# The tightest width table of the AUGRU: one line or two

## The chip, the cores and the metric

The kernel runs on one core of one Trainium2 chip. The metric is the device time of one execution in microseconds (us), the median of several runs. The kernel before takes 2072.88 us (three runs, 2072.65 to 2073.33). One execution was also recorded by the hardware profiler; its span, from the first to the last instruction, is 2067.4 us.

## What is computed

The reference scores 1024 users, each with a history of up to 100 items of 128 numbers. A GRU runs over all 100 steps of every history, an attention over the GRU's states gives one weight per user and step, and a second recurrence, the AUGRU, runs over the GRU's states with these weights. A small network makes one score of the AUGRU's state at the last real step of the user. Cut to the part that matters here:

```python
def augru_step(h, inp):
    x_t, a_t = inp
    ti = jnp.concatenate([h, x_t], axis=-1)
    r = jax.nn.sigmoid(ti @ aug_Wr.T + aug_br)
    u = jax.nn.sigmoid(ti @ aug_Wu.T + aug_bu)
    h_hat = jnp.tanh(jnp.concatenate([h * r, x_t], axis=-1) @ aug_Wh.T + aug_bh)
    u = a_t[:, None] * u
    h_new = (1.0 - u) * h + u * h_hat
    return (h_new, h_new)
...
idx = (sequential_length - 1).astype(jnp.int32)[:, None, None]
attention_feature = jnp.take_along_axis(aug_out, idx, axis=1)[:, 0, :]
```

Only the state at step `sequential_length - 1` is read. A user whose history has 40 items needs no AUGRU step after the fortieth. The lengths are drawn evenly from 1 to 100, so the number of users still alive falls by about 10 per step.

## The kernel before, in words

All data are f32, and the 128 features lie on the partitions. The users are two halves of 512 columns. The kernel has two phases.

The first phase (`gru_phase`, the first 1450 us) does the GRU, the attention and the sums over the history, step by step for both halves. Between its steps a generator, `load_later`, does small preparations one piece at a time. One of them ranks the users by length. The AUGRU then takes users in order of falling length, dealt alternately to the two halves, so that the living users are always the first columns of both halves.

The second phase (`augru_phase`, from about 1450 us to the end) is the AUGRU. Its loop runs over t from 1 to 99 and over the two halves i. Each turn (`half_step`) works on the first `widths[t]` columns of its half. Per turn TensorE does six matmuls of that width: three that open the gates of a turn to come with the GRU states (L1044) and three that close gates with the state or the reset state (L1048). ScalarE does three activations (L1056, L1068, L1069), VectorE five elementwise operations (L1072, L1074, L1076, L1082, L1085) and one transpose of the keys for t+2 in blocks of 32 columns (L1034). Steps 0 to 7 get their keys through TensorE transposes instead (L1030). The order of all instructions is written out by hand.

The keys of later steps come by indirect DMA from GpSimd (`load_rows`, L164). Eight steps are fetched at a time, in blocks of 32 columns, as many as cover the width at the first of the eight steps. Each fetch is preceded by a one-column copy (L163) that waits for a result of the loop and so paces the fetches. `spread` deals the fetches of the next eight steps over the turns before them. As groups of 64 columns die, `predict(g)` does the last network for them; its pieces run between the turns.

The widths are constants of the program. They come from a straight line that lies above the number of living users:

```python
EIGHTH, FALL, LEAST = 8, 41, 96
SPARE = (10, 40)
ROOM = [[EIGHTH * (HB + n) - FALL * t for t in range(T)] for n in SPARE]
ALIVE = [[min(HB, 2 * -(-r // (2 * EIGHTH))) for r in room] for room in ROOM] + [[HB] * T]
WIDTHS = [[max(LEAST, n) for n in alive] for alive in ALIVE]
```

A line is kept in eighths of a column: it starts `n` columns above 512 and falls 41/8 columns a step. The width is the line's value rounded up to an even number, at most 512 and at least 96. There are three tables: room for 10 more columns per half, room for 40, and full width. The program holds the whole AUGRU three times, once per table. `load_later` counts the living users of every step with eight small matmuls (L311), compares the counts with both lines, which GpSimd wrote with two iota instructions (L274), and stores a number, `over`. After the first phase the kernel loads it and branches (L1246 on) to the tightest table whose line lies nowhere below the count.

Of the kernel before, what the change touches and what calls it, by code (L numbers as in the profile page):

```python
# [9 lines left out]
F32 = mybir.dt.float32  # L10
BF16 = mybir.dt.bfloat16
I32 = mybir.dt.int32
# [9 lines left out]
T = 100  # L22
HB = 512
NH = B // HB
# [35 lines left out]
GATHER = 70  # L60


EIGHTH, FALL, LEAST = 8, 41, 96
SPARE = (10, 40)
ROOM = [[EIGHTH * (HB + n) - FALL * t for t in range(T)] for n in SPARE]
ALIVE = [[min(HB, 2 * -(-r // (2 * EIGHTH))) for r in room] for room in ROOM] + [[HB] * T]
WIDTHS = [[max(LEAST, n) for n in alive] for alive in ALIVE]

# [6 lines left out]
def kernel(ctx: ExitStack, tc: tile.TileContext, a: dict, out: bass.AP):  # L75
# [26 lines left out]
    nc = tc.nc  # L102
# [9 lines left out]
    over_d = dram.tile([1, 1], I32, name="over_d")  # L112
# [63 lines left out]
    def gru_phase(pools):  # L176
# [10 lines left out]
        pre = pools.enter_context(tc.tile_pool(name="pre", bufs=1))  # L187
# [52 lines left out]
        def load_later():  # L240
# [28 lines left out]
            ids = pre.tile([P, NG, 2], I32, name="ids")  # L269
            nc.gpsimd.iota(ids[:, :, 0], pattern=[[P, NG]], base=0, channel_multiplier=1)  # L270
            rooms = []
            for n in SPARE:
                rooms.append(pre.tile([1, T], I32, name=f"room_i{n}"))
                nc.gpsimd.iota(  # L274
                    rooms[-1],
                    pattern=[[-NH * FALL, T]],
                    base=NH * EIGHTH * (HB + n),
                    channel_multiplier=0,
                )
            yield  # L280
            length = pre.tile([P, NG], F32, name="length")
            nc.scalar.copy(length, len_i)
# [2 lines left out]
            own = pre.tile([P, NG], F32, name="own")  # L285
            nc.scalar.copy(own, ids[:, :, 0])
            room = []
            for n, room_i in zip(SPARE, rooms):
                room.append(pre.tile([1, T], F32, name=f"room{n}"))
                nc.scalar.copy(room[-1], room_i)  # L290
            yield

# [17 lines left out]
            for g in range(NG):  # L310
                nc.tensor.matmul(  # L311
                    count, lhsT=ones, rhs=alive[:, g, :], start=g == 0, stop=g == NG - 1
                )
            over = pre.tile([1, len(SPARE)], F32, name="over")
            for j in range(len(SPARE)):
                nc.vector.scalar_tensor_tensor(
                    out=room[j],
                    in0=count,
                    scalar=float(EIGHTH),
                    in1=room[j],  # L320
                    op0=ALU.mult,
                    op1=ALU.is_gt,
                )
                nc.vector.tensor_reduce(over[:, j : j + 1], room[j], AX.X, ALU.max)
# [12 lines left out]
                pattern=[[1, B]],  # L337
                base=0,
                channel_multiplier=0,
# [300 lines left out]
        def blocked(t):  # L640
            return t.rearrange("p (k r) -> p k r", r=R)
# [156 lines left out]
        def nothing():  # L798
            pass

        rest = load_later()
        early = [load_rows(0, i, HB, mid) for i in range(NH)]
        more_early = [load_rows(1, i, HB, kx) for i in range(NH)]

        late, again, early_from = 6, 24, 84
        for s in range(T):
            last = s == T - 1
            n, due = divmod(s - again, 4)
            n, i = divmod(n, NH)
# [85 lines left out]
        n = ENDS[-3] - ENDS[-4] + 1  # L895
# [33 lines left out]
        for half in reversed(halves):  # L929
            t = blocked(s_bs[NH * (soft["j"] % 2) + half.i])  # L930
# [311 lines left out]
        with ExitStack() as pools, tc.manual_schedule():  # L1242
            augru_phase(pools, WIDTHS[n], ALIVE[n])

    over = nc.values_load(over_d, min_val=0, max_val=len(SPARE))
    with tc.If(over < 1) as fits:  # L1246
        augru(0)
    with fits.Else():
# [70 lines left out]
```

## Time and profile before

| what | value |
|---|---|
| median time | 2072.88 us |
| profiled span | 2067.4 us |
| TensorE (PE) busy | 2029.8 us, 98% |
| VectorE (DVE) busy | 1755.2 us, 85% |
| GpSimd (POOL) busy | 1304.8 us, 63% |
| ScalarE (ACT) busy | 831.5 us, 40% |
| DMA | 99 GB/s on average |
| mean granted TensorE clock | 0.996 |
| first turn of the AUGRU loop starts | 1466.92 us |
| last turn of the AUGRU loop (t=99, second half) starts | 2054.11 us |

Busy time is the time in which an engine had at least one instruction in work. The ends of matmuls are modelled and neighbours overlap, so the busy share of PE does not say how near PE is to its limit; the distance between the starts of matmuls does. PEld is TensorE's loading of weights, which runs beside the matmuls. Each f32 matmul appears in the trace as two records, each with its own weight load. In the group lists, "+47 forms" means that other shapes are averaged in.

### The profile page before, as it was taken

The numbers are of one execution on the slowest core, as the hardware profiler recorded it, in microseconds if no ns is written. First come the engines' busy times: TensorE is split into PE (matmuls) and PEld (weight loads), VectorE is DVE, ScalarE is ACT, GpSimd is POOL, SyncE is SP. The second block draws the span as 40 slices with busy tenths as digits, with TensorE's granted clock in tenths as the row PEclk, the third lists the DMA queues.
The fourth block names the chain that finished last, engine by engine and source line by source line (L and its number), as shares of the span: only waits on it lengthen the run. The fifth ranks groups of instructions, "written<-read, shape, count | busy, mean of one in ns | idle before, by whom it ended". The sixth has DMA issues, their size and how long they took to land. (4 is left out here: it accounts for less than half of the span.)

```text
span 2067.4 us, 26811 instructions
## 1 busy us (share of the span) xinstructions
PE 2029.8 (98%) x8320; PEld 978.9 (47%) x8320; DVE 1755.2 (85%) x3050; ACT 831.5 (40%) x1516; POOL 1304.8 (63%) x1306
## 2 busy tenths in 40 slices
PE   8999999999999999999999999997899999999997
PEld 3343333333333333333333333333444556679997
DVE  6888999998989898988889899999467777888886
ACT  3334343333434343334334343343344444445554
POOL 0234939669796959595987767998545434444332
PEclk9999999999999999999999999999999999999999
DMA  4543333323334333333432332333434333333332
GB/s 119 116 93 94 98 103 97 102 80 88 110 111 101 112 114 113 105 111 102 122 97 77 95 104 88 103 104 104 113 103 110 98 91 98 94 97 102 88 75 36
DMA packets 254324, 205.09 MB, mean 99 GB/s; under 512 B 75814, under 2 KB 216842, under 8 KB 254170
## 3 DMA queue, kind: packets, MB, share of 16 engines
q1 hardware_dynamic: 240266, 170.64, 29.6%
q0 software_dynamic: 12320, 32.44, 5.7%
q8 instruction: 68, 1.11, 0.2%
q14 instruction: 86, 0.70, 0.1%
q10 hardware_dynamic: 1584, 0.20, 0.1%
HBM read 147.16 MB, written 54.40 MB: 97 GB/s over the span
## 5 line engine op out<-in xcount | busy, mean ns | idle before, releaser
L495 PE MATMUL ps<-x,wih 128*128 128x512 f32 x1200 | 592.1, 603 | 4.0 <-DMA x<-in_hist_x 4.0
L495 PE MATMUL ps<-hn,whh 128*128 128x512 f32 x1188 | 574.4, 592 | 0.0
L495 PEld LDWEIGHTS ps<-x,wih 128*128 128x128 f32 x1200 | 220.7, 190 | 327.1 <-issue 251.4
L495 PEld LDWEIGHTS ps<-hn,whh 128*128 128x128 f32 x1188 | 225.7, 190 | 284.1 <-issue 276.0
L481 POOL TENSOR_TENSOR xm<-x,m 128x512 f32<-128x512 f32 x200 | 247.1, 1236 | 136.3 <-DMA m<-mask_d 136.0
L526 ACT ACTIVATE ps<-ps,bih 128x512 f32<-128x512 f32 x200 | 132.4, 662 | 488.7 <-DVE ps L525 488.7
L507 ACT ACTIVATE r<-ps,brz 128x512 f32<-128x512 f32 x200 | 137.4, 687 | 371.1 <-PE ps L495 370.2
L482 POOL TENSOR_TENSOR hist<-hist,xm 128x512 f32<-128x512 f32 x200 | 266.6, 1333 | 15.7
L594 POOL TENSOR_TENSOR pooled<-pooled,kw 128x512 f32<-128x512 f32 x191 | 254.3, 1332 | 15.0
L593 POOL TENSOR_TENSOR kw<-kt,e 128x512 f32<-128x512 f32 x191 | 219.1, 1147 | 64.7 <-DVE e L766 64.6
L164 POOL DMA_INDIRECT rows<-keys_d,idx_k x208 | 202.0, 971 | 82.2 <-POOL rows L163 52.7
L570 DVE TENSOR_TENSOR kq<-hn,item 128x512 f32<-128x512 f32 x200 | 228.5, 1182 | 0.0
L657 PE MATMUL pm<-hn,wk 128*32 128x512 f32 x1200 | 211.9, 596 | 3.7 <-ACT q L238 2.2
L657 PE MATMUL pm<-kq,wkq 128*32 128x512 f32 x1200 | 209.5, 592 | 0.0
L1056 ACT ACTIVATE c<-ph,bh 128x96 f32<-128x96 f32 (+42 forms) x198 | 96.7, 489 | 257.1 <-PE ph L1048 227.4
L657 PE MATMUL pm<-mv,w 128*32 128x512 f32 (+1 forms) x808 | 196.3, 598 | 1.4 <-DVE e L747 1.4
L163 POOL COPY rows<-rest 128x1 f32<-128x1 f32 x208 | 39.1, 188 | 210.1 <-DVE rest L1085 205.0
L691 DVE TENSOR_TENSOR f<-pm,q 128x512 f32<-128x512 f32 x200 | 128.4, 683 | 50.5 <-PE pm L657 50.4
L1072 DVE TENSOR_TENSOR pu<-pu,c 128x96 f32<-128x96 f32 (+42 forms) x197 | 88.8, 451 | 92.9 <-ACT c L1056 80.3
L530 DVE TENSOR_TENSOR d<-hn,ps 128x512 f32<-128x512 f32 x198 | 136.1, 687 | 34.9 <-ACT ps L526 32.5
L525 DVE TENSOR_TENSOR ps<-ps,u 128x512 f32<-128x512 f32 x200 | 140.0, 700 | 21.6 <-PE ps L495 0.5
L531 DVE TENSOR_TENSOR d<-ps,d 128x512 f32<-128x512 f32 x200 | 138.3, 691 | 23.5 <-ACT ps L527 6.5
(180 smaller groups left out, 3024.5 us busy)
## 6 DMA issues: line engine op xcount, KB each, us to landing
x<-in_hist_x SPq DMA_DIRECT2D x212, 256.0 KB
keys_d<-kt SPq DMA_DIRECT2D x46, 1024.0 KB
m<-mask_d SPq DMA_DIRECT2D x200, 128.0 KB
keys_d<-kt SPq DMA_DIRECT2D x64, 64.0 KB
rows<-keys_d,idx_k POOLq DMA_INDIRECT x208
s_b<-mv SPq DMA_DIRECT2D x200, 8.0 KB
mask_i<-in_mask SPq DMA_DIRECT2D x8, 200.0 KB
at<-att_d SPq DMA_DIRECT2D x32, 48.0 KB
```

The lines of the kernel that those rows point to most:

```text
L164: nc.gpsimd.indirect_dma_start(out=r[:, k, :], out_offset=None, in_=keys_d[q], in_offset=bass.IndirectOffsetOnAxis(ap=idx_k[:, k, i : i + ...
L481: nc.gpsimd.tensor_mul(d, x, m)
L482: nc.gpsimd.tensor_add(acc, acc, d)
L495: nc.tensor.matmul(p, lhsT=w[:, g, :], rhs=v, start=(j == 0), stop=(j == len(parts) - 1),)
L507: nc.scalar.activation(r, pr, AF.Sigmoid, bias=brz[:, 0:1])
L525: nc.vector.tensor_add(pi, pi, u)
L530: nc.vector.tensor_sub(d, h, pi)
L531: nc.vector.tensor_mul(d, pz, d)
L570: nc.vector.tensor_mul(kq, h, item[:, self.cols])
L593: eng.tensor_mul(d, k, w)
L594: eng.tensor_add(acc, acc, d)
L657: nc.tensor.matmul(p[i][s, :], lhsT=w[:, s], rhs=v, start=start, stop=stop)
```

## The change

The tightest table is made of two lines instead of one. From step 0 the first line starts only 2 columns above 512 and falls 38/8 columns a step. From step 16 on a second line takes over, the old one moved down from 10 to 8 columns of room. The second table (40 columns) and the third stay. The purpose is to spend fewer columns on users that have ended. The lines are written by GpSimd as before, now with one iota per piece. Two columns of room for both halves together are what is left at the tightest place: at step 56, 464 of the given users are alive and the two halves have 466 columns of line.

```diff
-EIGHTH, FALL, LEAST = 8, 41, 96
-SPARE = (10, 40)
-ROOM = [[EIGHTH * (HB + n) - FALL * t for t in range(T)] for n in SPARE]
+EIGHTH, LEAST = 8, 96
+
+LINES = (((0, 2, 38), (16, 8, 41)), ((0, 40, 41),))
+ROOM = [
+    [max((t0, EIGHTH * (HB + n) - fall * t) for t0, n, fall in lines if t0 <= t)[1] for t in range(T)]
+    for lines in LINES
+]
 ALIVE = [[min(HB, 2 * -(-r // (2 * EIGHTH))) for r in room] for room in ROOM] + [[HB] * T]
...
             rooms = []
-            for n in SPARE:
-                rooms.append(pre.tile([1, T], I32, name=f"room_i{n}"))
-                nc.gpsimd.iota(
-                    rooms[-1],
-                    pattern=[[-NH * FALL, T]],
-                    base=NH * EIGHTH * (HB + n),
-                    channel_multiplier=0,
-                )
+            for j, lines in enumerate(LINES):
+                rooms.append(pre.tile([1, T], I32, name=f"room_i{j}"))
+                ends = [t0 for t0, _, _ in lines[1:]] + [T]
+                for (t0, n, fall), t1 in zip(lines, ends):
+                    nc.gpsimd.iota(
+                        rooms[-1][:, t0:t1],
+                        pattern=[[-NH * fall, t1 - t0]],
+                        base=NH * (EIGHTH * (HB + n) - fall * t0),
+                        channel_multiplier=0,
+                    )
```

What this does to the widths of the first table, per half:

| steps t | width before | width after | columns less per step | sum |
|---|---|---|---|---|
| 0 | 512 | 512 | 0 | 0 |
| 1, 2, 3 | 512, 512, 508 | 510, 506, 500 | 2, 6, 8 | 16 |
| 4 to 8 | 502 to 482 | 496 to 476 | 6 | 30 |
| 9 to 12 | 476 to 462 | 472 to 458 | 4 | 16 |
| 13, 14, 15 | 456, 452, 446 | 454, 448, 444 | 2, 4, 2 | 8 |
| 16 to 83 | 440 to 98 | 438 to 96 | 2 | 136 |
| 84 to 99 | 96 | 96 | 0 | 0 |
| all | 27580 | 27374 | | 206 |

Everything that depends on a width follows: the matmuls, activations and elementwise operations get narrower; at steps 8, 14, 33, 58, 64 and 83 the keys need one block of 32 less; the fetch that begins at step 8 has 15 blocks instead of 16 per half and the one at step 64 has 6 instead of 7. The groups of 64 columns numbered 7, 3 and 1 die one step earlier, at t=13, 63 and 88, so their `predict` pieces move one step forward. No instruction is added or removed on PE, DVE or ACT; GpSimd gets one iota more and, within the branch that is taken, four fetches and four pacing copies less.

More of the change, by code (lines that the diff above doesn't have):

```diff
@@ L287, in load_later @@
             room = []
-            for n, room_i in zip(SPARE, rooms):
-                room.append(pre.tile([1, T], F32, name=f"room{n}"))
+            for j, room_i in enumerate(rooms):
+                room.append(pre.tile([1, T], F32, name=f"room{j}"))
                 nc.scalar.copy(room[-1], room_i)
@@ L313, in load_later @@
                 )
-            over = pre.tile([1, len(SPARE)], F32, name="over")
-            for j in range(len(SPARE)):
+            over = pre.tile([1, len(LINES)], F32, name="over")
+            for j in range(len(LINES)):
                 nc.vector.scalar_tensor_tensor(
@@ L1243, in augru @@
             augru_phase(pools, WIDTHS[n], ALIVE[n])
-    over = nc.values_load(over_d, min_val=0, max_val=len(SPARE))
+    over = nc.values_load(over_d, min_val=0, max_val=len(LINES))
     with tc.If(over < 1) as fits:
```

## The prediction

> **What bounds the kernel now.** I read the busy shares first, then the places where PE stood idle in the AUGRU loop, then the starts of single matmuls, because busy shares alone do not tell what a narrower matmul is worth. From the page of the kernel before:
>
> ```profile
> PE 2029.8 (98%) x8320; PEld 978.9 (47%) x8320; DVE 1755.2 (85%) x3050; ACT 831.5 (40%) x1516; POOL 1304.8 (63%) x1306
> ```
>
> PE looks full. The waits of PE in the loop, 1480 to 2055 us, say that almost nothing holds it up visibly:
>
> ```profile
> PE pu L1044 <- ACT c L1056: 1.6, 2, 1.1
> PE pu L1044 <- issue: 0.5, 1, 0.5
> PE ph L1048 <- issue: 0.2, 1, 0.2
> ```
>
> 2.3 us of idle time in 575 us. But is PE streaming columns, or loading weights, or keeping step with a chain that the modelled ends hide? The busy times of two stretches of the loop (the columns are PE, PEld, DVE, ACT, POOL, then clock, DMA share, GB/s) show that the answer differs:
>
> ```profile
> 1480.00:1960.00 480.00, 479.27 (x1747) 314.06 (x1746) 378.34 (x805) 220.83 (x434) 222.68 (x378) 1.00 0.38 102
> 1960.00:2055.00 95.00, 92.41 (x758) 89.50 (x757) 80.08 (x358) 54.44 (x192) 29.06 (x46) 1.00 0.32 60
> ```
>
> Up to 1960 us DVE has 21% free and the weight loads 35%; after it the weight loads fill 94% and DVE 84%. The timeline of PE (start, duration) gives the length of a turn as the distance between two starts of `pr<-h,wr`:
>
> ```profile
> 1581.98 0.94 PE L1048 MATMUL pr<-h,wr 128*128 128x462 f32 x2
> 1582.76 0.94 PE L1048 MATMUL pu<-h,wu 128*128 128x462 f32 x2
> ...
> 1586.63 0.94 PE L1048 MATMUL pr<-h,wr 128*128 128x462 f32 x2
> ...
> 1918.33 0.53 PE L1048 MATMUL pr<-h,wr 128*128 128x216 f32 x2
> 1920.52 0.53 PE L1048 MATMUL pr<-h,wr 128*128 128x216 f32 x2
> ...
> 1986.98 0.39 PE L1048 MATMUL pr<-h,wr 128*128 128x128 f32 x2
> 1988.48 0.38 PE L1048 MATMUL pr<-h,wr 128*128 128x124 f32 x2
> ...
> 2017.62 0.39 PE L1048 MATMUL pr<-h,wr 128*128 128x96 f32 x2
> 2019.00 0.39 PE L1048 MATMUL pr<-h,wr 128*128 128x96 f32 x2
> ```
>
> A turn at 462 columns takes 4.65 us, one at 216 takes 2.19: slope 2.46/246 = 0.0100 us per column and turn. Six matmuls of 462 columns at the 0.78 us between the first two starts make 4.68, the whole turn: there PE streams without a gap, and the line goes through zero. At 128 columns a turn takes 1.50, at 96 it takes 1.38: slope 0.12/32 = 0.00375. There the turn hangs on weight loads and on the chain from matmul to activation to DVE and back.
>
> I followed the distances through all 99 steps. A step (two turns) equals 0.020 us times its width to within 0.05 us from step 6 to step 71 (160 columns: 3.50 against 3.20 with a `predict` piece in it), except where `predict` pieces add matmuls and at steps 66 and 67. Steps 2 to 5 add the L1030 transposes (11.16 for 10.24 at step 2), which are PE work too. From step 72 on steps lie above that line (154 columns: 3.23 for 3.08; 112: 2.90 for 2.24), and the narrow slope holds.
>
> **What the skill says.** The Trainium skill, "FP8 and Floating Point Precision", TensorE Precision Notes: a true FP32 matmul is 4 passes through the array. "TensorE: Matmul & The Clock Gate", Back-to-back issue gap: a pass of N columns takes about N/2.4 ns plus 2.5. Four passes of 462 give 0.780 us; the trace has 0.78. So a column costs 4/2.4 = 1.67 ns per matmul, twelve matmuls per step 0.0200 us, which the measured slope confirms. The same page, LDWEIGHTS, prices a load of 128 columns at 107 ns; two per matmul make 0.21 us, and the trace has matmuls 0.22 us apart at 96 to 128 columns: narrower matmuls gain nothing there by themselves. "Trace Analysis", Identifying the Most-Contended Engine: matmul busy time is not a measure of nearness to the limit; the 97% of PE at 1960 us and later, where starts hardly depend on width, agrees. "Runtime: NRT & Kernel Launch", Instruction fetch mechanics: each engine's instructions are fetched in blocks by its own DMA queue, mostly hidden. The page shows these queues but no wait that names them, so the trace can't decide it.
>
> **The change part by part.**
>
> *Columns, steps 2 to 71.* 206 columns go in all. Step 1 has 2, steps 72 to 83 have 24, so 180 remain. 180 x 0.0200 = 3.60 us. Slope and starts bound this between 3.5 and 3.7.
>
> *Columns, steps 72 to 83.* 24 x 2 x 0.00375 = 0.18 us. Bounds: 0 if weight loads alone set the turn, 0.48 at the wide slope.
>
> *Step 1.* Two columns, 0.04 us if PE streamed. But this step took 13.28 us for 10.24 of loop matmuls and waits for attention weights and transposes, so 0 to 0.04; I take 0.02.
>
> *ACT and DVE.* Their operations get shorter by some 2 ns each; in the wide part PE hides it (DVE at 79%), in the narrow part it is inside the measured slope. Six fewer 32-column blocks in the DVE transposes (twice each) are hidden the same way.
>
> *Fetches.* Four pacing copies and fetches leave POOL, 4 x (0.19 + 0.97) = 4.6 us of POOL time. No DVE wait for a fetched row appears in the loop, so nothing waits for them and they are worth 0. Where a fetch waits for its pacing result, only other fetches and `predict`'s two DMAs queue behind it on POOL; the latter have slack of many us.
>
> *One more iota.* The two of before took 201 ns each at 5.1 us; POOL's next work starts at 67.34 us. A third costs about 0.2 us inside 62 us of idle time: 0.
>
> *Moved `predict` pieces.* Same matmuls, one step earlier, in the same place between turns: 0, with perhaps 0.1 either way.
>
> Sum: 3.60 + 0.18 + 0.02 = 3.80 us, or 0.18%. 2072.88 - 3.80 = 2069.08, rounded 2069.1 us. The line for "faster by 0.2%" is 2068.73.
>
> **What is not fixed by the sum: stalls.** Some steps are longer than their neighbours' law by amounts without a width in them: step 66 by 1.66 us (5.38 for 3.72), 67 by 0.40, 73 by 1.89 (5.06 for 3.17), 91 by 1.04, and 76, 84, 85 and 97 by 0.2 to 0.4 each: some 6.1 us. In them an activation starts late though its input is ready, and the wait is put down to issue or to a matmul long ended. This looks like late instructions, and these meet other DMA traffic. Narrower steps shift the meeting points, so a third of the 6.1 us, 2 us, may come or go.
>
> **The rivals.**
>
> *The stalls shrink too.* Two fewer fetches in front of step 64 and two in front of step 8 mean less traffic, and the stall at 66 lies shortly behind. 2069.1 - 2.0 = 2067.1. Against it: the fetches running during step 66 are those for step 72, whose number is unchanged.
>
> *The stalls grow, or another engine takes part of the gain.* DVE at 79% in the wide part leaves a fifth free and PE never waits for it there, so a new bound is unlikely; stalls that land badly are the likelier form: 2069.1 + 2.0 = 2071.1.
>
> *The second table is taken.* If one count lay above the new line, the branch would go to the table with 40 columns of room. It has 1992 columns more than the table of before in steps 2 to 71 and 442 in the rest: 1992 x 0.0200 + 442 x 0.0075 = 43.2 us, so 2116 us, slower. For it: room for both halves together falls to 2 columns at step 56. Against it: the lengths are given with the inputs, and counted step by step none exceeds the line (464 of 466 at the tightest); the line's whole numbers are exact.
>
> **How the numbers follow.** The sum as it stands, with stalls within 1 us of before (2068.1 to 2070.1): 0.48. Stalls shrink: 0.30. Stalls grow: 0.18. Second table, or stalls growing by 8 us: 0.04. Faster by over 0.2%: all of the second case and the third of the first that lies below 2068.73, 0.30 + 0.17 = 0.47. Within 0.2%: the rest of the first and the third, 0.31 + 0.18 = 0.49. Slower: 0.04. The range reaches to both stall cases: 2066.9 to 2071.3; left out are the second table and the ends of the stall cases.
>
> **What would show it.** In the profile after, a turn at 458 columns (step 12) should take 4.61 us where 462 took 4.65; the loop from step 2 to step 72 should be 3.6 us shorter apart from stalls; steps from 84 on should be unchanged at 2.77; POOL should show 204 fetches L164 where there were 208. Starts of equal width further apart than before, or form names such as 128x506 missing, would make it wrong.

## The result and the profile after

The changed kernel takes 2065.86 us (median of 6 runs, 2063.26 to 2066.81). The kernel before took 2074.08 us beside it (6 runs, 2072.65 to 2076.91). The ratio is 0.9958, with a 95% interval of 0.9945 to 0.9971: about 8.2 us or 0.42% faster. Forecast were 2069.1 us and a range of 2066.9 to 2071.3. The direction held, but the time lies below the range, with a gain of more than twice the 3.8 us worked out.

In some sessions (a session is a set of runs taken together) both kernels run some 8 to 12 us faster than in others, the kernel before near 2062 us instead of near 2073 us, so the comparisons below are between runs of one session unless the text says otherwise; the first measurement belongs to the level of 2073 us.

The page of the changed kernel, busy times, and its row of key fetches:

```profile
PE 2027.4 (98%) x8320; PEld 980.1 (47%) x8320; DVE 1753.7 (85%) x3050; ACT 829.9 (40%) x1516; POOL 1300.6 (63%) x1299
...
L168 POOL DMA_INDIRECT rows<-keys_d,idx_k x204 | 198.4, 973 | 82.3 <-POOL rows L167 49.3
```

PE, DVE and ACT have as many instructions as before, POOL has seven fewer (1306 to 1299: eight go, one iota comes), and there are 204 fetches where there were 208, as the diff says. The waits of PE in most of the loop (1480 to 2045 us), and two starts of step 12 in the timeline of PE:

```profile
PE ph L1054 <- issue: 1.2, 3, 0.6
PE ph L1054 <- DVE r L1080: 0.7, 2, 0.5
```

```profile
1583.23 0.93 PE L1054 MATMUL pr<-h,wr 128*128 128x458 f32 x2
1587.84 0.93 PE L1054 MATMUL pr<-h,wr 128*128 128x458 f32 x2
```

A turn of 458 columns takes 4.61 us, the number forecast, and the form 128x458 says that the new table was taken. PE still waits for almost nothing in this view. The two profiled spans, 2065.0 and 2067.4 us, differ by 2.4 us only, less than the medians. This is no contradiction. The profiled run of before took 2069.16 us, 3.7 us less than the median of 2072.88 that stood beside it, and the profiled run of after, 2066.8 us, was among the longest of its six. In its trace the first turn of the loop starts 2.2 us later than in the trace of before (1469.08 against 1466.92 us), and this hides a part of the gain.

Where do the 8 us come from, if the sum makes 3.8? Two theories were tested. **Columns**: a column is worth 0.020 us per step in steps 2 to 71 and 0.0075 in steps 72 to 83, and nothing else changes; 8 us would be scatter. **Stalls**: the changed program also has smaller stalls, run after run. A stall here is the time by which a step is longer than its width and its `predict` pieces explain.

### The profile page after: what moved, and what is told of

Its sections match the earlier page's. It is cut to its first block, busy times and chain, and to the rows that moved or that the text cites. A ratio compares the mean times of both kernels' runs of the same rounds, so it can differ in the third digit from the quotient of the medians.

```text
span 2065.0 us, 26800 instructions
## 1 busy us (share of the span) xinstructions
PE 2027.4 (98%) x8320; PEld 980.1 (47%) x8320; DVE 1753.7 (85%) x3050; ACT 829.9 (40%) x1516; POOL 1300.6 (63%) x1299
## 5 line engine op out<-in xcount | busy, mean ns | idle before, releaser
L1062 ACT ACTIVATE c<-ph,bh 128x96 f32<-128x96 f32 (+41 forms) x198 | 96.5, 488 | 253.4 <-PE ph L1054 221.2
L1078 DVE TENSOR_TENSOR pu<-pu,c 128x96 f32<-128x96 f32 (+41 forms) x197 | 88.2, 448 | 91.2 <-ACT c L1062 75.5
```

## The experiments

### The kernel before against itself, and the change taken apart

The two lines of the new table were tried one at a time, beside the changed kernel and the kernel before.

```diff
# first_line
-LINES = (((0, 2, 38), (16, 8, 41)), ((0, 40, 41),))
+LINES = (((0, 2, 38), (16, 10, 41)), ((0, 40, 41),))
# late_line
-LINES = (((0, 2, 38), (16, 8, 41)), ((0, 40, 41),))
+LINES = (((0, 10, 41), (16, 8, 41)), ((0, 40, 41),))
```

The kernel before itself:

> The kernel before against itself: it shows how far two sets of runs of one program lie apart. Columns theory (a column is worth 0.020 us per step, the rest of the measured gain of 8 us is scatter from run to run): ratio 1.000, single runs scattered over 4 us or more. Stall theory (the changed program has smaller stalls, run after run): ratio 1.000 too, but with single runs within 2 us, so that 8 us cannot be scatter.

The changed kernel:

> The changed kernel once more, in the same session as the parts. Columns theory: 3.8 us less than before (ratio 0.9982). Stall theory: 7 to 9 us less (0.996) again.

The first line alone:

> Only the first line of the change: 70 columns less, all in steps 1 to 15, and two fetches less in front of step 8; from step 16 on as before. Columns theory: 68 x 0.020 + 0.02 = 1.4 us less. Stall theory, if the fetches in front of step 8 or the shape of the program matter: 3 us less or more.

The second line alone:

> Only the second line of the change: 136 columns less, 2 in each of steps 16 to 83, and two fetches less in front of step 64; the first 16 steps as before. Columns theory: 112 x 0.020 + 24 x 0.0075 = 2.4 us less. Stall theory, if the fetches in front of step 64 are what shortens the stalls behind it: 6 us less or more.

Measured, with the kernel before at 2062.28 us beside them:

| kernel | median us | ratio, 95% interval | start of step 2 to start of step 72, us | step 72 to last step, us |
|---|---|---|---|---|
| before, again | 2062.94 | 1.0004 (0.9995 to 1.0012) | 485.37 | 81.07 |
| first line | 2061.33 | 0.9995 (0.9987 to 1.0003) | 484.04 | 81.03 |
| second line | 2059.97 | 0.9989 (0.9982 to 0.9995) | 483.17 | 80.90 |
| both (the change) | 2058.39 | 0.9984 (0.9976 to 0.9992) | 481.84 | 80.85 |

The last two columns are distances between starts of `pr<-h,wr` in the timeline of PE, from one trace of each kernel. For the kernel before here:

```profile
1478.48 1.02 PE L1048 MATMUL pr<-h,wr 128*128 128x512 f32 x2
...
1963.85 0.42 PE L1048 MATMUL pr<-h,wr 128*128 128x154 f32 x2
...
2044.92 0.39 PE L1048 MATMUL pr<-h,wr 128*128 128x96 f32 x2
```

and for the changed kernel beside it:

```profile
1478.53 1.01 PE L1054 MATMUL pr<-h,wr 128*128 128x506 f32 x2
...
1960.37 0.42 PE L1054 MATMUL pr<-h,wr 128*128 128x152 f32 x2
...
2041.22 0.39 PE L1054 MATMUL pr<-h,wr 128*128 128x96 f32 x2
```

From the first to the second start is 1963.85 - 1478.48 = 485.37 us before and 1960.37 - 1478.53 = 481.84 after: 3.53 us less, forecast 3.60. From the second to the third it is 81.07 and 80.85: 0.22 less, forecast 0.18. The first line alone takes 1.33 off the wide steps (68 x 0.020 = 1.36), the second 2.20 (112 x 0.020 = 2.24); together they are the 3.53 of the change. So at this level the columns theory holds term by term in the loop, and the whole gain is 3.9 us. The medians of the parts fit the forecasts (1.0 us for 1.4, and 2.3 us for 2.4), though the first line alone can't be told from no change.

### More columns

```diff
-LINES = (((0, 2, 38), (16, 8, 41)), ((0, 40, 41),))
+LINES = (
+    (
+        (0, 1, 40), (8, 2, 44), (16, -8, 37), (24, 4, 42), (32, -21, 36), (40, -16, 37),
+        (48, 13, 42), (56, 50, 47), (64, -6, 40), (72, -5, 40), (80, -47, 36), (88, 29, 43),
+    ),
+    ((0, 40, 41),),
+)
```

> The tightest table made of twelve lines, one per eight steps, each as low as the counts of living users allow: 606 columns less than before (534 in steps 2 to 71, 68 in steps 72 to 83), 400 less than after the change. Nothing of the computation is left out. Columns theory: 534 x 0.020 + 68 x 0.0075 + 0.05 = 11.2 us less than before (ratio 0.9946), 7.4 less than after. Stall theory, with the gain made by the changed program and not by the columns: about as much as after, not three times as much.

The changed kernel and the kernel before were run beside it:

> The changed kernel against the kernel before. Columns theory: 3.8 us less wherever it runs, ratio 0.9982. If the larger gain of the first measurement belongs to a chip, and these runs fall on such a chip: 7 to 9 us less, and the kernel before is then above 2070 us.

> The kernel before once more, for a second trace of it beside the three others. The columns theory says nothing of it. Stall theory: where a chip shows steps that are longer than their width and their extra matmuls explain (66, 67, 73, 91 and others in the first trace, 6 us in all), they lie in the same steps again; on a chip without them the loop is free of them, as in the other four traces.

Measured: the kernel before 2061.74 us, itself again 2062.09 (ratio 0.9999, 0.9990 to 1.0008), the change 2058.06 (0.9982, 0.9974 to 0.9990), twelve lines 2050.85 (0.9943, 0.9930 to 0.9957). Three times the columns give three times the gain: 10.9 us against 11.2 forecast, steps 2 to 71 taking 474.90 us instead of 485.37 (10.47 us less, 534 x 0.020 = 10.68). This version beats both kernels. It is fitted to these lengths as closely as the lines allow; lengths that exceed a line would take the next table.

### Fetches left out

```diff
         def gathers(q):
             for i in range(NH):
+                if q > 3:
+                    rows[q, i] = rows[q - 2, i]
+                    continue
                 yield from load_rows(q, i, widths[FIRST[q]], kp)
```

> The kernel before with the fetches of key rows for step 24 and later left out: the later steps use the rows that are there, so their keys are the wrong ones and only the time counts. Columns theory: widths are those of before and nothing waits for a fetch, so no change on a chip without stalls, within 0.5 us. Stall theory: if this chip shows stalls and they come from fetches in the way of instruction loads, they go, up to 6 us less; if they stay, the fetches are not their cause.

Measured: 2068.1 us, 6.4 us more (ratio 1.0031, 1.0020 to 1.0042), where no change was expected. It is not the loop: steps 2 to 71 take 485.56 us and the rest 81.60, together 0.7 us more than before. About 5 us lie behind the loop. From the start of the last turn to the end of the span are 18.4 us (2048.79 to 2067.2) where the kernel before has 13.4 (2046.75 to 2060.1). The trace shows where: among the last instructions of the program is a long `DRAIN` of GpSimd's sequencer, and the span ends 0.8 us after it. The views of that source line give the shortest, the middle and the longest of its three `DRAIN`s in ns, first in the kernel before in the same session, then with the fetches left out:

```profile
L1315 POOLq DRAIN  x3: 40/107/3737, 2055.5 to 2059.8; - x3
```

```profile
L1318 POOLq DRAIN  x3: 40/107/8968, 2057.4 to 2066.9; - x3
```

It takes 8.97 us instead of 3.74, which is 5.2 of the 6.4 us. The same instruction depends on the number of fetches in the other traces too, but the other way round: 3.74 us in every trace with the 208 fetches of the kernel before, 3.57 with the 206 of either line alone, 3.41 with the 204 of the change, 3.25 with the 202 of twelve lines. Why 148 fetches less lengthen it while two less shorten it by 0.16 us is not shown. For the change it means that the four fetches saved are worth nothing in the loop, as forecast, but 0.33 us at the end of the program. As the session showed no stalls, this run says nothing of their cause.

### Other sessions

The first measurement had not been met again, so the pair was run in two more sessions.

> The kernel before once more, for its trace and level on whatever chip these runs fall on. If the kernel before lies above 2070 us there, as in the first measurement, the loop should show several us of steps that are too long, and different ones in different runs; if it lies near 2062 us, none.

> The changed kernel beside it. Columns theory: 3.8 us less, ratio 0.9982, on any chip. Theory of the chip: 7 to 9 us less where the kernel before lies above 2070 us, 3.8 us where it lies near 2062 us.

Measured: before 2062.10 us, itself again 2061.82, the change 2057.78 (ratio 0.9978, 0.9969 to 0.9987).

> The kernel before, for its level and trace on the chip of the next three kernels. Where it lies above 2070 us the steps 66, 67, 73 and 91 are too long again; where it lies near 2062 us no step is.

> The changed kernel beside it: 7 to 9 us less where the kernel before lies above 2070 us, with long steps at 65, 67, 75 and 90 instead; 3.8 us less where it lies near 2062 us.

Measured: before 2062.67 us, itself again 2062.70, the change 2058.14 (0.9978, 0.9970 to 0.9987). Four sessions at this level give 3.9, 3.7, 4.3 and 4.5 us, and the traces of one kernel in these sessions agree step by step within 0.01 us from step 2 on: there are no stalls in them that come and go. Scatter among these sessions does not make 8 us out of 4, so the level of 2073 us was the next thing to look at.

### One more load per turn

```diff
             if t + 2 < T:
                 load_key(t + 2, i)
+            extra = sp.tile([P, P], F32, name="extra")
+            nc.sync.dma_start(out=extra, in_=a["hist_x"][t][:, ts(i, P)])
```

> The kernel before with one more load of 64 KB per turn of the AUGRU loop into a tile that nobody reads; nothing of the computation changes. Traffic theory of the stalls (instruction loads come late when other transfers are in their way): steps without a predict piece become too long here and there, 2 us or more in all. If traffic of this size has nothing to do with the stalls: the loop stays within 0.5 us of the kernel before, each step at its law.

> The changed kernel with the same extra load per turn. Columns theory: 3.8 us less than the kernel before with the extra load. If stalls appear and the change makes them smaller: 6 us less or more.

The kernel before took 2073.60 us beside them. With the extra loads it took 2074.86 (ratio 1.0006, 0.9998 to 1.0015), so 64 KB more per turn change nothing that can be told. The changed kernel with them took 2066.27 (median of 5): 8.6 us less than its partner. The gain of 8 us is thus real and repeats where the kernel before lies near 2073 us. The traces show stalls: compared step by step with the traces at 2062 us, the loop from step 2 on is 11.3 us longer in the kernel before with loads and 8.4 us in the changed one, 2.9 us less.

### An engine's instructions shifted

```diff
             exponents()
+            if 20 <= s < 68:
+                nc.scalar.copy(pad[:, 1:2], pad[:, 0:1])
```

The second kernel has `nc.gpsimd.memset(pad[:, 1:2], 0.0)` in that place. In both, the small tile `pad` is made and zeroed once at the start.

> The kernel before with 48 one-column copies on ScalarE, one per step of GRU steps 20 to 67, where ScalarE is idle for more than half of the time; all widths as before. Where the kernel before lies near 2062 us: the same within 0.5 us. Where it lies above 2070 us: if the long steps belong to places in the instruction stream of ScalarE, they move some 8 steps forward (48 instructions at 6 per step) and the time changes by 2 us or more; if they belong to something else, they stay at 66, 67, 73 and 91.

> The kernel before with 48 one-column writes on GpSimd in the same GRU steps; all widths as before. Where the kernel before lies near 2062 us: the same within 0.5 us. Where it lies above 2070 us: if the long steps belong to places in the instruction stream of GpSimd, they move or change by 2 us or more; if not, they stay at 66, 67, 73 and 91.

Measured at the level of 2062 us: 2062.31 and 2062.04 us against 2062.67 (ratios 0.9998 and 0.9997): no change, but this level has no stalls to move. Both were run again in another session:

> The kernel before with 48 one-column copies on ScalarE, one per step of GRU steps 20 to 67, again. Where the kernel before lies near 2062 us: the same within 0.5 us. Where it lies above 2070 us: if the long steps belong to places in ScalarE's instruction stream, they leave steps 66, 67, 73 and 91 and the time changes by 2 us or more; if not, they stay there.

> The kernel before with 48 one-column writes on GpSimd in the same GRU steps, again. Where the kernel before lies near 2062 us: the same within 0.5 us. Where it lies above 2070 us: if the long steps belong to places in GpSimd's instruction stream, they move or change by 2 us or more; if not, they stay at 66, 67, 73 and 91.

Beside them the kernel before now took 2074.01 us, and the shifted kernels 2073.62 and 2073.52 us (0.9998, 0.9989 to 1.0007, and 0.9999, 0.9990 to 1.0008): no change again. Nor did the longest steps move. Microseconds by which a step is longer than the same step of the same program in the traces near 2062 us:

| step | before, first profile | before, ScalarE shifted | before, GpSimd shifted | before, extra loads | after, first profile | after, extra loads |
|---|---|---|---|---|---|---|
| 60 | 0.0 | 0.52 | 0.54 | 0.94 | 0.0 | 0.0 |
| 65 | 0.0 | 0.0 | 0.0 | 0.0 | 0.85 | 0.83 |
| 66 | 1.66 | 3.95 | 3.63 | 3.65 | 0.0 | 0.0 |
| 67 | 0.41 | 0.0 | 1.68 | 0.0 | 1.07 | 2.10 |
| 73 | 1.89 | 1.76 | 1.74 | 2.00 | 0.0 | 0.0 |
| 75 | 0.0 | 0.0 | 0.0 | 0.0 | 0.59 | 0.0 |
| 76 | 0.0 | 0.37 | 0.57 | 0.33 | 0.10 | 0.58 |
| 83 | 0.14 | 0.51 | 0.53 | 0.54 | 0.21 | 0.51 |
| 90 | 0.0 | 0.0 | 0.0 | 0.0 | 1.22 | 1.24 |
| 91 | 1.01 | 1.12 | 1.15 | 1.40 | 0.0 | 0.0 |
| all from 2 on | 5.96 | 10.78 | 11.43 | 11.26 | 5.38 | 8.36 |

The largest stalls belong to the program: steps 66, 73 and 91 are long in all four forms of the kernel before and in no trace of the changed one, 65 and 90 the other way round. Others come and go (60, 67 and 75 in the table; 84, 88 and 97 beside it), and step 83 is long in both programs. Shifting ScalarE's or GpSimd's stream ahead of the branch into the AUGRU does not move the large ones. What such a step looks like is seen best in the timeline of ACT around step 66, first in the kernel before against itself at the level of 2062 us, then with ScalarE's stream shifted at the level of 2073 us (in brackets the idle time ahead of the activation and what ended it):

```profile
1943.20 0.41 ACT L1056 ACTIVATE c<-ph,bh 128x184 f32<-128x184 f32 x1 [0.80 <-PE ph L1048]
1945.05 0.41 ACT L1056 ACTIVATE c<-ph,bh 128x184 f32<-128x184 f32 x1 [0.78 <-PE ph L1048]
```

```profile
1945.32 0.42 ACT L1060 ACTIVATE c<-ph,bh 128x190 f32<-128x190 f32 x1 [1.60 <-PE pu L1052]
1950.45 0.41 ACT L1060 ACTIVATE c<-ph,bh 128x184 f32<-128x184 f32 x1 [3.91 <-remote]
```

and what PE and ACT waited for in that run, PE in the loop (1480 to 2060 us), ACT at 1930 to 1960 us:

```profile
PE pu L1048 <- ACT c L1060: 2.7, 1, 2.7
PE pu L1048 <- issue: 1.4, 2, 0.8
```

```profile
ACT c L1060 <- PE ph L1052: 7.4, 9, 0.9
ACT c L1060 <- remote: 3.9, 1, 3.9
```

ACT normally idles 0.8 us before this activation; here it idles 3.91 us, though by the modelled end its matmul was long done. PE then stands still behind it, because its next gate waits for this activation, as the waits of PE say. At the level of 2062 us the same instruction in the same step is on time.

Late instructions are not what is seen here. For the ten us around the stall (1943 to 1953 us) the DMA view of this run lists two queues, and none of those that carry instructions:

```profile
q0 software_dynamic: 313, 0.82, 30.3%
q1 hardware_dynamic: 443, 0.27, 12.6%
```

"Remote" only means that no instruction was matched to the semaphore update that released the activation. The kept trace also holds the times of these updates, and the semaphore that the activation waits for is one that only PE's matmuls update. An update of it lies at 1950.42 us and the activation starts at 1950.45. The same 0.02 us lie between update and start where the activation is on time, so it is PE's update that comes late. It comes 3.7 us after the start of the matmul's second record (1946.71 us), where a run without the stall has 0.34 us. In the long steps PE's updates come 0.7 us or more apart where they are otherwise 0.3 us apart, and then several at once (1950.42, 1950.47, 1950.51, 1950.57). Pairs of them less than 0.06 us apart do not occur in the loop in any of the 14 traces from sessions at the level of 2062 us, and 24 to 37 times in each of the six at the level of 2073 us. The six traces also hold fewer of PE's updates in the loop, 914 to 970 instead of 1117 to 1134, so some went unrecorded. Whether a matmul ends late or only its update is held back can't be read, as the ends of matmuls are modelled; whether the recording of the updates has a part in it was not tried.

## Why the prediction was wrong

**What bounds the loop: right.** Steps 2 to 71 follow the sum of their matmuls' columns. Forecast were 3.60 us, measured 3.53 to 3.54 us in four sessions at the level of 2062 us, each from one trace of either kernel. The formula N/2.4 + 2.5 ns that the prediction took from the Trainium skill ("TensorE: Matmul & The Clock Gate", Back-to-back issue gap) is given there for an isolated matmul, beside a measured 131 ns at 512 columns for a stream. This stream fits the formula: matmuls of 512 columns start 0.86 us apart (1480.20 and 1481.06 us in step 2 of the first trace), 215 ns for each of the four passes.

**The narrow steps: right in size.** From step 72 to the last, 0.12 to 0.23 us in the same four pairs of traces instead of 0.18. The 0.02 us of step 1 can't be read: in these pairs that step is 0.03 to 0.62 us longer after the change, so it varies by more than its two columns are worth.

**The parts costed at nothing: right in the loop, not behind it.** Narrower activations and DVE work, the fetches and the moved `predict` pieces leave nothing over beyond the columns at the level of 2062 us. Behind the loop the four fetches are worth the 0.33 us by which the `DRAIN` is shorter. With it the sum is 4.1 us, and the four sessions gave 3.7 to 4.5. The iota was not measured by itself; PE's starts up to GRU step 94 agree within 0.3 us in both first traces. One chance was summed a little too high: of the first case's 2.0 us only 0.63 lie below 2068.73, which makes 0.15 if the case is spread evenly, and not 0.17. Nothing hangs on it.

**The failed step: the stalls.** The prediction put 6.1 us of stalls beside the sum, took them as unchanged in its likeliest case, and let "a third of the 6.1 us, 2 us, may come or go". Both numbers were too small for the level of its own base. The 6.1 us were read from one trace, and that run took 2069.16 us, the shortest of the kernel before at this level. The typical one has some 11.5 us of them: 2073.6 us against 2062.1, and 10.8 to 11.4 us more in the loop in three other traces. The changed kernel has about 7.8 us: 2065.9 against 2058.1, and 8.4 us in the loop of the trace with extra loads. So the change takes away some 3 to 4 us of stalls on top of some 4 us of columns and fetches. The 3.7 us between 11.5 and 7.8 come from medians of different sessions, the 2.9 us between 11.3 and 8.4 from one pair of traces of one session. The two first traces show only 0.6 us of it (5.96 and 5.38), because the run of before was an unusually short one. The rival "the stalls shrink too" is the case that came true; its end of the range, 2066.9 us, was 1 us too high. At the level of 2062 us, without stalls, the sum alone would have been enough.

**Its mechanism did not hold either.** The prediction read the stalls as late instructions that meet other DMA traffic. Around the largest stall no instruction queue moved a packet, and the activation started 0.02 us after an update of PE's semaphore that came late itself. More traffic and shifted streams of two engines changed neither the time nor the place of the large stalls.

**Why they shrink is open.** The rival argued with two fewer fetches in front of step 64; the kernel with fetches left out was not run at the level of 2073 us, so this was not tested, and that the rival had the direction right is luck as far as the runs show. After the change the stalls of 1.7 to 4.0 us at step 66 and 1.7 to 2.0 us at step 73 are gone, 0.8 us appear at 65, 1.1 to 2.1 us lie at 67, and the one at 91 has moved to 90. The stalls may go with `predict`: in the two first traces GpSimd's fetch for a group that has died (`part`) starts in steps 66 and 90 before and in steps 64 and 89 after, in or just ahead of long steps. But the same fetches in steps 13, 27, 40 and 52 leave no long step, and moving `predict` alone was not tried. What holds up PE's updates, and why a session is at one level or the other, stays open too.

**The other rivals fell.** The second table was not taken (the forms show the new widths), DVE did not become the bound (PE waits for it for 0.7 us in the loop), and the stalls did not grow.

## What to carry to other kernels

In a stretch where the starts of matmuls follow their width with a line through zero, a column removed is worth its share of the matmuls' time, here 0.020 us per step, and nothing more or less; this held to 0.1 us for either part of the change and the whole, and to 0.2 us for three times the change. Before a fixed stall is read from one trace, compare that run's own time with the median: here the profiled run was 3.7 us faster, and its stalls were about half of the usual. Where a wait is put down to nothing that fits, look at when the semaphore was updated, and not only at when the instruction ahead is said to end. And when a small edit gains more than its sum, repeat the pair in other sessions before looking for a cause in the edit.

## What had not been expected of the hardware

The same program took near 2062 us in four sessions and near 2073 us in three (one chip showed both), and the difference lies in few steps of the loop, the largest in the same places each time for one program, with the granted clock of the two kernels at 0.994 to 0.996 in either. In these steps PE's semaphore updates come late, 3.4 us in the longest stall, and several at once. The passage from the GRU to the AUGRU, from the start of GRU step 94 (counted from 0) to the first turn of the loop, varies by 2.9 us from trace to trace of the changed kernel (139.3 to 142.3 us). And a `DRAIN` behind the loop takes 3.25 to 3.74 us with 202 to 208 fetches but 8.97 us with 60.
